# A separate order for the last visit of a two-layer graph kernel, and seven products for one output

## The chip, the cores and the metric

The kernel runs on one core of a Trainium2 chip. The metric is the device time in microseconds; 2795.61 is the median of three runs (2795.58 to 2795.65). A profiled execution of the same kernel took 2798.83.

## The reference

Sixty-four graphs of 256 nodes with 512 features go through two layers, all in fp32. Layer 0 is a graph attention with 8 heads of 64 units, layer 1 an attention with 8 heads whose weights are mixed with the adjacency. After each layer the input is added and the sum is normalized.

```python
# layer 0
feats = jnp.einsum('bnf,hfu->bhnu', X, W)
dense = leaky_relu(e_self[..., :, None] + e_neigh[..., None, :], 0.2) + NEG_BIG * (1.0 - A)
out = relu(einsum('bhij,bhju->bhiu', softmax(dense), feats) + b)
x = _layernorm(x + out)
# layer 1
qkv = (x @ W_qkv).reshape(B, N, HEADS, 3, DIM_HEAD)
attn = softmax(where(m2, q @ k.T * scale, -big)) * LA
attn = attn + LG * adj + LD * jnp.exp(-dist)     # adj and dist are both the adjacency
out = (attn @ v) @ W_out + b_out
x = _layernorm(x + out)
```

## The kernel before

Each graph is split in two row tiles of 128 nodes (T = 2) and four feature blocks of 128 (C = 4). Work of a graph is cut into stages (`turned`, `proj0`, `attend0`, `proj1`, `softmax1`, `attend1`), and each stage into named steps. `do(stage, graph, step)` (line 1240) emits one step and then calls `in_order`, which ties every instruction to the one before it on its engine. So the order of the `do` calls is the order of every engine's queue; nothing reorders it later.

Four graphs are in flight. For each graph b from 2 to 63 two functions are called: `attention0_beside_projections1` (line 1460) runs layer 0's attention of graph b beside the q/k and value projections of graph b-1 and the weighting of b-2; `attention1_beside_projections0` (line 1545) runs the rest of layer 1 of b-2, the scores of b-1 and layer 0's projections of b+1. After the loop `end` (line 1598) finishes graphs 60 to 63. For b = 63 the steps of the nonexistent graph 64 are skipped by `do`, so the loop's last visit keeps the loop's order with holes in it.

A projection is a 2 x 2 block product done in seven products instead of eight (`seven`, line 328). The products p1, p6, p7, p4 share one PSUM bank: each adds to it, and after each of them ScalarE (ACT) copies the bank out (`COPIES`, line 325), so the next of the four waits for that copy. p2 has a bank alone; p5 and p3 share one. VectorE (DVE) adds these banks to the copies (`add`: 11 after p1 and p2, 22 after p7 and p5, 12 after p3), and p3 must wait for the add 22 that reads its bank. The left factors of the seven products are differences of blocks (`left_factors`, line 307; for the output they are made in `half_blocks`, line 1116). All matmuls of a product go through `halved` (line 83), which writes 64 output rows at a time; row 87 of the profile is therefore shared by `pq_p` (q and k), `pv_p` (values), `pf_p` (layer 0) and `po_p` (output). The scores `pz` use 64 input rows (line 951), the row sums `pd` 32 output rows (line 988), `common` and `recs` the full array.

In layer 1 the exponentials run on ACT (line 972). The pair sums `both` run on DVE, row sums on TensorE (PE), and `invert` and `inverted` make reciprocals. A write to DRAM and a broadcast load bring them back as `rb` (1 MB, line 1039). `weights` (lines 1059 and 1068) then multiplies the exponentials by them and adds the common part. `values` (line 1078) multiplies with the value rows and ACT copies the result to `oT`. The last graph skips the broadcast: `last_values` computes the unscaled product `raw` and the part `common` apart, and `last_scaled` spreads the reciprocals with a matmul (`recs`).

In `end` of the kernel before, the output of graph 62 is not done in seven products but by rows: `project(t)` (line 1193) makes four blocks by two column groups for each row tile, then `sum_up` adds the input rows. Graph 63 does the same. The normalization takes the mean and three small operations on POOL (lines 385, 402, 405, 406), squares (391) and the scaling (410) on ACT, then a store on SP. `rows_again` (line 1088) loads the input rows of a graph back into `y`; graph 61's use the buffer of graph 60's output and so wait for its store. Buffers are tagged: one tag with `bufs=n` is a ring of n, and a step waits until the older user of its slot is done; `mm` (four PSUM slots) and `sc` (two large PSUM slots) are those that matter here.

Of the kernel before, what the change touches and what calls it, by code (L numbers as in the profile page):

```python
# [8 lines left out]
FT = mybir.dt.float32  # L9
# [8 lines left out]
def kernel(  # L18
# [49 lines left out]
    work = ctx.enter_context(tc.tile_pool(name="work", bufs=2))  # L68
# [858 lines left out]
    PROBS, REC = {}, {}  # L927

    def softmax1(b):
# [4 lines left out]
        both = {}  # L934
# [3 lines left out]
        def scores(g, part=None):  # L938

            if part is not None and part > 0:  # L940
                exponentials(g, PZ[g], {1: slice(0, None), 2: slice(0, -1), 3: slice(-1, None)}[part])
                return
            if g == 2 and b < NB - 1:
                pz = [ps_tile([P, T, N], f"pz_{b}_{g}_{r}") for r in range(2)]
            else:
                pz = psum.tile([P, 2, T, N], FT, tag="sc", name=f"pz_{b}_{g}", bufs=2)
                pz = [pz[:, r] for r in range(2)] + [pz]
            for j in range(T):
                for r in range(2):
                    rows = slice(r * U, (r + 1) * U)  # L950
                    matmul(  # L951
                        pz[r][:, j, :],
                        QK[b][rows, g, 1, j * P : (j + 1) * P],
                        QK[b][rows, g, 0, :],
                        start=True,
                        stop=True,
                    )
            if part == 0:
                PZ[g] = pz
                return  # L960
            exponentials(g, pz)
# [87 lines left out]
    def attend1(b):  # L1049
        if b < NB - 1:  # L1050
            oT = work.tile([P, C, N], FT, tag="oT", name=f"oT_{b}", bufs=1)
        else:
            oT = work.tile([P, C, N], FT, tag="xC", name=f"oT_{b}", bufs=1)
        av = {}

        def weights(g, step=None):
# [81 lines left out]
        def last_values():  # L1138

            raw = psum.tile([P, HG, N], FT, tag="sc", name="raw", bufs=2)  # L1140
            for g in range(HG):
                for j in range(T):
                    for r in range(2):
                        matmul(
                            raw[r * U : (r + 1) * U, g, :],
                            V1[b][:, j, 2 * g + r, :],
                            PROBS[b][g][:, r, j, :],
                            start=(j == 0),
                            stop=(j == T - 1),
                        )  # L1150
            for g in range(0, HG, 2):
                nc.scalar.copy(oT[:, g : g + 2, :], raw[:, g : g + 2, :])
            common = psum.tile([P, HG, N], FT, tag="sc", name="common", bufs=2)
            for g in range(HG):
                for j in range(T):
                    matmul(
                        common[:, g, :],
                        V1[b][:, j, 2 * g : 2 * g + 2, :].rearrange("p h u -> p (h u)"),
                        CT[b][:, j, :],
                        start=(j == 0),  # L1160
                        stop=(j == T - 1),
                    )
            LAST["common"] = common
            sel = work.tile([P, Q, U], FT, tag="gb", name="heads", bufs=1)
            nc.vector.tensor_copy(sel, ident[:, 0:P:B].unsqueeze(2).to_broadcast([P, Q, U]))
            LAST["sel"] = sel

        def last_scaled():

            for i in range(HG // 2):  # L1170
                both = slice(2 * i, 2 * i + 2)
                pr = ps_tile([P, 2, N], f"recs_{i}")
                for q in range(2):
                    matmul(
                        pr[:, q, :],
                        LAST["sel"][:, 2 * q : 2 * q + 2, :].rearrange("p k u -> p (k u)"),
                        REC[b][:, i, :],
                        start=True,
                        stop=True,
                    )  # L1180
                nc.vector.tensor_mul(oT[:, both, :], pr, oT[:, both, :])
                nc.vector.tensor_add(
                    oT[:, both, :], LAST["common"][:, both, :], oT[:, both, :]
                )

        def residual():
            if b == NB - 1:
# [20 lines left out]
        def store(ts=None):  # L1208
# [11 lines left out]
            residual=residual,  # L1220
            values=values,
            last_values=last_values,
            last_scaled=last_scaled,
            project=project,
            rows_again=rows_again,
# [234 lines left out]
    def attention0_beside_projections1(b):  # L1460
# [28 lines left out]
                do("attend0", b, "product", g, t)  # L1489
        do("attend0", b, "rec0", 0)  # L1490
        do("attend0", b, "rec0", 1)
        if b == 2:
            do("turned", 3, "xT")
            do("turned", 3, "xC")
# [103 lines left out]
    def end():  # L1598

        b = NB - 1  # L1600
        do("proj1", b, "qk", "p1")
# [8 lines left out]
        do("proj1", b, "qk", "p2")  # L1610
        do("proj1", b, "qk_add", 11)
        do("proj1", b, "qk", "p6")
# [8 lines left out]
        do("attend1", b - 1, "weights", 2)  # L1621
        do("attend1", b - 1, "weights", 3)
        do("attend1", b - 1, "values", 0)
        do("attend1", b - 1, "values", 1)
        do("attend1", b - 2, "residual")
        do("attend1", b - 2, "sum_up", 0)
        do("attend1", b - 2, "sum_up", 1)
        do("softmax1", b, "scores", 0)
        do("softmax1", b, "both", 0)
        do("softmax1", b, "scores", 1)  # L1630
        do("softmax1", b, "both", 1)
        do("proj1", b, "values", "p1")
        do("attend1", b - 2, "squares")
        do("attend1", b - 1, "residual")
        do("attend1", b, "residual")
        do("proj1", b, "values", "p2")
        do("proj1", b, "v_add", 11)
        do("attend1", b - 1, "values", 2)
        do("attend1", b - 1, "values", 3)
        do("softmax1", b, "scores", 2)  # L1640
        do("softmax1", b, "both", 2)
        do("softmax1", b, "scores", 3)
        do("softmax1", b, "both", 3)
        do("proj1", b, "values", "p6")
        do("attend1", b - 2, "store")
        do("proj1", b, "values", "p5")
        do("proj1", b, "values", "p7")
        do("proj1", b, "v_add", 22)
        do("proj1", b, "values", "p4")
        do("proj1", b, "values", "p3")  # L1650
        do("proj1", b, "v_add", 12)
        do("softmax1", b, "sums")
        do("softmax1", b, "invert")
        do("softmax1", b, "inverted")
        do("attend1", b, "last_values")
        do("attend1", b, "last_scaled")
# [4 lines left out]
        tiles = [slice(t, t + 1) for t in range(T)]  # L1661
# [62 lines left out]
```

## Time and profile before

| | us |
|---|---|
| median of the runs | 2795.61 |
| profiled execution, its own time | 2798.83 |
| its span, first to last instruction | 2796.9 |
| PE busy | 2778.1 (99%) |
| DVE busy | 2561.5 (92%) |
| ACT busy | 1794.7 (64%) |
| POOL busy | 417.0 (15%) |

The chain of work that ended last lies on PE for 97% of the span. A visit of the loop repeats about every 43 us: the first q/k product of a graph starts at 2649.70 for one and at 2692.39 for the next. The change begins at about 2705 us, after the last layer-0 attention product, so everything up to there is the same in both kernels. In a timeline row the columns are start, busy time, engine, line, operation, output and inputs, tile and number of records, and in brackets the idle time before it with what ended it. A matmul instruction leaves two records.

### The profile page before, as it was taken

How to read it: one execution, taken by the hardware profiler on the slowest of the kernel's cores; microseconds unless marked ns; L12 is line 12 of the kernel's file. 1: busy time of each engine (PE TensorE's matmuls, PEld its weight loads, DVE VectorE, ACT ScalarE, POOL GpSimd, SP SyncE). 2: the span in 40 equal slices, each digit the busy share in tenths (PEclk: the TensorE clock that was granted, in tenths of full speed). 3: DMA queues.
4: the chain of work that ended last, by engine and by line, in shares of the span. 5: the costliest groups of instructions: out<-in, count | busy, mean ns of one | idle time of the engine just before them, and what ended most of it. 6: DMA issues, size and time to landing. Idle time of an engine off the chain costs nothing.

```text
span 2796.9 us, 93442 instructions
## 1 busy us (share of the span) xinstructions
PE 2778.1 (99%) x38584; PEld 2201.3 (79%) x38584; DVE 2561.5 (92%) x5264; ACT 1794.7 (64%) x5051; POOL 417.0 (15%) x1031
## 2 busy tenths in 40 slices
PE   9999999999999999999999999999999999999998
PEld 7778778778788788888787877877877878778775
DVE  7899999999999999999999999999999999999984
ACT  4666666666666666666666666666666666666663
POOL 1111111111111111111111111111111111111111
PEclk9999999999999999999999999999999999999999
DMA  6444544545545445444454454454454544544531
GB/s 142 124 110 133 141 124 139 126 133 146 123 128 140 119 138 140 124 139 124 134 146 122 129 140 122 135 140 125 139 123 135 142 123 132 140 118 139 137 107 67
DMA packets 778388, 362.56 MB, mean 130 GB/s; under 512 B 694767, under 2 KB 696303, under 8 KB 761966
## 3 DMA queue, kind: packets, MB, share of 16 engines
q1 hardware_dynamic: 775854, 356.07, 47.7%
q8 instruction: 306, 5.01, 0.7%
q14 instruction: 116, 0.95, 0.1%
q10 hardware_dynamic: 2112, 0.52, 0.1%
HBM read 288.11 MB, written 68.13 MB: 127 GB/s over the span
## 4 chain that ended last, share of the span: by engine, by line
PE 97%; DVE 1%; ACT 1%; DMA 0%; issue 0%; POOL 0%; SPq 0%; DVEq 0%; POOLq 0%
PE pq_p L87 27%; PE po_p L87 14%; PE pf_p L87 13%; PE pv_p L87 13%; PE av L790 9%; PE pz L951 8%; PE av L1078 8%; PE pd L988 2%; PE po L87 1%; PE pf L87 0%; DVE p L1059 0%; DMA gb<-gs 0%; DVE p L1068 0%; PE pg L663 0%; ACT x L811 0%
## 5 line engine op out<-in xcount | busy, mean ns | idle before, releaser
L87 PE MATMUL pq_p<-hC,wqk_sb 128*64 128x128 f32 x8192 | 470.4, 273 | 1.7 <-ACT qk L348 1.5
L87 PEld LDWEIGHTS pq_p<-hC,wqk_sb 128*64 128x64 f32 x8192 | 448.7, 137 | 3.5 <-ACT qk L348 2.2
L767 DVE SCALAR_TENSOR_TENSOR pT<-gb,ccol,at 128x256 f32<-128x256 f32 x992 | 403.0, 478 | 17.2 <-ACT ccol L677 17.2
L87 PE MATMUL pq_p<-hT,wqk_sb 128*64 128x128 f32 x6144 | 357.9, 273 | 0.0
L972 ACT ACTIVATE p<-pz,hide 128x512 f32<-128x512 f32 x638 | 337.9, 621 | 30.3 <-PE pz L951 30.3
L87 PEld LDWEIGHTS pq_p<-hT,wqk_sb 128*64 128x64 f32 x6144 | 342.2, 137 | 9.8 <-issue 0.8
L1059 DVE TENSOR_TENSOR p<-p,rb 128x1024 f32<-128x1024 f32 x252 | 299.0, 1207 | 3.9 <-DMA rb<-rs 3.9
L1068 DVE TENSOR_TENSOR p<-p,ct 128x1024 f32<-128x1024 f32 x252 | 299.4, 1208 | 0.2
L811 ACT ACTIVATE x<-av,rec 128x64 f32<-128x64 f32 x1024 | 223.9, 334 | 62.2 <-DVE rec L803 62.2
L790 PE MATMUL av<-v,pT 128*64 128x65 f32 x8192 | 253.7, 222 | 1.7 <-issue 1.1
L87 PE MATMUL pf_p<-wf_sb,xC 128*64 128x264 f32 x1984 | 254.0, 386 | 0.1
L725 ACT ACTIVATE v<-v 128x64 f32<-128x64 f32 x1024 | 251.2, 336 | 3.8 <-DVE v L716 3.7
L790 PEld LDWEIGHTS av<-v,pT 128*64 128x64 f32 x8192 | 249.6, 138 | 4.2 <-issue 2.9
L402 POOL TENSOR_SCALAR rstd_l<-rstd_l 128x2 f32<-128x2 f32 (+1 forms) x130 | 95.0, 731 | 1054.9 <-ACT junk L391 1054.8
L87 PE MATMUL pv_p<-wv_sb,hC 128*64 128x256 f32 x2048 | 245.9, 381 | 2.4 <-ACT v L348 2.4
L348 ACT COPY qk<-pq_p 128x512 f32<-128x512 f32 x256 | 148.8, 581 | 154.6 <-PE pq_p L87 151.2
L348 ACT COPY v<-pv_p 128x256 f32<-128x256 f32 x256 | 95.4, 373 | 223.6 <-PE pv_p L87 223.5
L951 PE MATMUL pz<-qk 64*128 64x256 f32 x2048 | 238.6, 383 | 0.0
L87 PE MATMUL po_p<-wo_sb,oC 128*64 128x256 f32 x1984 | 235.3, 379 | 0.0
L1078 PE MATMUL av<-p,v 128*64 128x256 f32 x2016 | 229.4, 379 | 2.1 <-DVE p L1068 2.1
L951 PEld LDWEIGHTS pz<-qk 64*128 64x128 f32 x2048 | 192.4, 186 | 44.9 <-issue 24.8
L980 DVE SCALAR_TENSOR_TENSOR both<-p 128x512 f32<-128x512 f32 x256 | 172.9, 677 | 41.5 <-ACT p L972 41.3
(175 smaller groups left out, 4549.0 us busy)
## 6 DMA issues: line engine op xcount, KB each, us to landing
rb<-rs SPq DMA_DIRECT2D x63, 1024.0 KB
gb<-gs SPq DMA_DIRECT2D x62, 1028.0 KB
hs<-x SPq DMA_DIRECT2D x64, 512.0 KB
xb<-in_x_dram SPq DMA_DIRECT2D x252, 128.0 KB
x<-in_x_dram SPq DMA_DIRECT2D x63, 512.0 KB
y<-hs SPq DMA_DIRECT2D x63, 512.0 KB
out_dram<-y SPq DMA_DIRECT2D x63, 512.0 KB
hb<-hs SPq DMA_DIRECT2D x248, 128.0 KB
```

What stands on the lines that cost most here:

```text
L87: matmul(dst[cols], lhsT[:, cols], rhs, **flags)
L348: nc.scalar.copy(out[COPIES[p]], dst)
L725: nc.scalar.activation(v[:, :U], v[:, :U], AF.Copy, scale=v[:, U : U + 1])
L767: nc.vector.scalar_tensor_tensor(pT[h][:, j, :], GB[b][h], CCOL[b][:, j, h : h + 1], AT[b][:, j, :], op0=ALU.max, op1=ALU.mult,)
L790: matmul(av[r * half : (r + 1) * half, k, :], pT[h][:, j, i : i + half], V0[b][:, j, h, :UA], start=(j == 0), stop=(j == T - 1),)
L811: nc.scalar.activation(X1[b][:, t, h * U : (h + 1) * U], av[:, k, :U], AF.Copy, scale=REC0[g][:, t, k : k + 1],)
L951: matmul(pz[r][:, j, :], QK[b][rows, g, 1, j * P : (j + 1) * P], QK[b][rows, g, 0, :], start=True, stop=True,)
L972: nc.scalar.activation(to, of, AF.Exp, bias=hide[:, j, b : b + 1], scale=U**-0.5)
L980: nc.vector.scalar_tensor_tensor(both[g], p[:, :, 0, :], TINY, p[:, :, 1, :], op0=ALU.add, op1=ALU.add)
L1059: nc.vector.tensor_mul(p, p, REC[b][:, k : k + 2, g // 2, :] .unsqueeze(2) .to_broadcast([P, 2, T, N]),)
L1068: nc.vector.tensor_add(p, p, CT[b].unsqueeze(1).to_broadcast([P, 2, T, N]))
L1078: matmul(av[0][r * U : (r + 1) * U, g % 2, :], V1[b][:, j, 2 * g + r, :], PROBS[b][g][:, r, j, :], start=(j == 0), stop=(j == T - 1),)
```

## The change

The loop ends at graph 62. For graph 63 only the first half is called, and it returns after the reciprocals of its attention. `end` then holds all that follows in an order of its own, in which the products of graphs 61, 62 and 63 alternate more finely. The output of graph 62 goes through `half_blocks` and the seven products (so `oT` of graph 63 takes the buffer tag `hC`, as `xC` now holds the differences for 62). The `common` part of graph 63 becomes a step of its own, `last_common`, ahead of the row sums, and `last_scaled` takes the half to do as an argument. Score block 2 of graph 63 uses two `mm` slots, as in the other graphs.

```diff
-            if g == 2 and b < NB - 1:
+            if g == 2:
                 pz = [ps_tile([P, T, N], f"pz_{b}_{g}_{r}") for r in range(2)]
...
-            oT = work.tile([P, C, N], FT, tag="xC", name=f"oT_{b}", bufs=1)
+            oT = work.tile([P, C, N], FT, tag="hC", name=f"oT_{b}", bufs=1)
...
-            common = psum.tile([P, HG, N], FT, tag="sc", name="common", bufs=2)
+
+        def last_common():
+
+            common = LAST["common"] = psum.tile([P, HG, N], FT, tag="sc", name="common", bufs=2)
...
-        def last_scaled():
-
-            for i in range(HG // 2):
+        def last_scaled(i):
...
         do("attend0", b, "rec0", 1)
+        if b == NB - 1:
+            return
...
     def end():
         b = NB - 1
+        tiles = [slice(t, t + 1) for t in range(T)]
+        do("attend1", b - 2, "weights", 0, 0)
+        do("attend1", b - 2, "weights", 1, 0)
+        do("attend1", b - 2, "weights", 0, 1)
...
+        do("proj1", b - 1, "values", "p7")
+        do("proj1", b - 1, "v_add", 22)
+        do("attend0", b, "squares", tiles[1], slice(0, 2))
+        do("attend1", b - 2, "weights", 2, 1)
+        do("attend1", b - 2, "weights", 3, 0)
+        do("softmax1", b - 1, "scores", 0, 0)
+        do("proj1", b - 1, "values", "p4")
+        do("proj1", b - 1, "values", "p3")
+        do("proj1", b - 1, "v_add", 12)
+        do("attend1", b - 2, "weights", 3, 1)
+        do("attend0", b, "norm")
+        do("proj1", b, "blocks")
+        do("softmax1", b - 1, "scores", 1, 0)
+        do("attend1", b - 2, "values", 0)
+        do("softmax1", b - 1, "scores", 0, 1)
+        do("attend1", b - 2, "values", 1)
+        do("softmax1", b - 1, "scores", 1, 1)
+        do("softmax1", b - 1, "scores", 2, 0)
+        do("attend1", b - 3, "residual")
+        for t in range(T):
+            do("attend1", b - 3, "sum_up", t)
...
+        do("softmax1", b - 1, "sums")
+        do("attend1", b - 2, "product_add", 22)
+        do("softmax1", b - 1, "invert")
+        do("proj1", b, "hT")
+        do("softmax1", b - 1, "inverted")
+        do("attend1", b - 2, "product", "p4")
+        do("attend1", b - 2, "product", "p3")
         do("proj1", b, "qk", "p1")
+        do("proj1", b, "hC")
+        do("attend1", b - 2, "product_add", 12)
         do("attend1", b - 3, "squares")
+        do("proj1", b, "qk", "p2")
+        do("proj1", b, "qk_add", 11)
+        do("proj1", b, "qk", "p6")
         do("attend1", b - 3, "store")
...
         do("attend1", b - 1, "weights", 1)
+        do("proj1", b, "values", "p1")
         do("proj1", b, "qk", "p4")
         do("proj1", b, "qk", "p3")
         do("proj1", b, "qk_add", 12)
         do("attend1", b - 1, "weights", 2)
+        do("proj1", b, "values", "p2")
+        do("proj1", b, "v_add", 11)
+        do("proj1", b, "values", "p6")
+        do("proj1", b, "values", "p5")
+        do("proj1", b, "values", "p7")
+        do("attend1", b - 2, "residual")
+        do("proj1", b, "v_add", 22)
...
         do("attend1", b - 1, "values", 0)
         do("attend1", b - 1, "values", 1)
+        do("proj1", b, "values", "p4")
+        do("proj1", b, "values", "p3")
+        do("attend1", b - 2, "squares")
         do("softmax1", b, "scores", 0)
+        do("softmax1", b, "scores", 1)
+        do("proj1", b, "v_add", 12)
+        do("softmax1", b, "scores", 2, 0)
+        do("attend1", b - 1, "values", 2)
+        do("attend1", b - 1, "values", 3)
...
+        do("attend1", b, "last_common")
+        do("softmax1", b, "sums")
+        do("softmax1", b, "invert")
+        do("attend1", b, "last_values")
+        do("softmax1", b, "inverted")
...
-        do("attend1", b - 1, "project", 0)
-        do("attend1", b - 1, "project", 1)
+        do("attend1", b - 1, "product", "p1")
+        do("attend1", b - 1, "product", "p2")
+        do("attend1", b - 1, "product_add", 11)
+        do("attend1", b - 1, "product", "p6")
+        do("attend1", b, "last_scaled", 0)
+        do("attend1", b - 1, "product", "p5")
+        do("attend1", b - 1, "product", "p7")
+        do("attend1", b - 1, "product_add", 22)
+        do("attend1", b, "last_scaled", 1)
+        do("attend1", b - 1, "product", "p4")
+        do("attend1", b - 1, "product", "p3")
+        do("attend1", b - 1, "product_add", 12)
+        for t in range(T):
+            do("attend1", b - 1, "sum_up", t)
         do("attend1", b - 1, "squares")
         do("attend1", b - 1, "store")
...
-    for b in range(2, NB):
+    for b in range(2, NB - 1):
         attention0_beside_projections1(b)
         attention1_beside_projections0(b)
+    attention0_beside_projections1(NB - 1)
     end()
```

More of the change, by code (lines that the diff above doesn't have):

```diff
@@ L1162, in last_values @@
                     )
-            LAST["common"] = common
             sel = work.tile([P, Q, U], FT, tag="gb", name="heads", bufs=1)
@@ L1166, in last_values @@
             LAST["sel"] = sel
-        def last_scaled():
-            for i in range(HG // 2):
[L1171 to L1183, printed above, removed]
-                )
+        def last_scaled(i):
+            both = slice(2 * i, 2 * i + 2)
+            pr = ps_tile([P, 2, N], f"recs_{i}")
+            for q in range(2):
+                matmul(
+                    pr[:, q, :],
+                    LAST["sel"][:, 2 * q : 2 * q + 2, :].rearrange("p k u -> p (k u)"),
+                    REC[b][:, i, :],
+                    start=True,
+                    stop=True,
+                )
+            nc.vector.tensor_mul(oT[:, both, :], pr, oT[:, both, :])
+            nc.vector.tensor_add(
+                oT[:, both, :], LAST["common"][:, both, :], oT[:, both, :]
+            )
         def residual():
@@ L1222, in attend1 @@
             last_values=last_values,
+            last_common=last_common,
             last_scaled=last_scaled,
@@ L1600, in end @@
         b = NB - 1
+        tiles = [slice(t, t + 1) for t in range(T)]
[3 more added lines that the diff above has]
+        for t in range(T):
+            do("attend0", b, "norm0", 0, t)
+        do("proj1", b - 1, "qk", "p4")
+        for t in range(T):
+            do("attend0", b, "norm0", 1, t)
+        do("proj1", b - 1, "qk", "p3")
+        do("attend1", b - 2, "weights", 1, 1)
+        do("proj1", b - 1, "qk_add", 12)
@@ new lines, in end @@
+        do("attend0", b, "end")
+        do("proj1", b - 1, "values", "p1")
+        do("proj1", b - 1, "values", "p2")
+        do("proj1", b - 1, "v_add", 11)
+        do("attend1", b - 2, "weights", 2, 0)
+        do("proj1", b - 1, "values", "p6")
+        do("attend0", b, "squares", tiles[0], False)
+        do("proj1", b - 1, "values", "p5")
+        do("proj1", b - 1, "values", "p7")
+        do("proj1", b - 1, "v_add", 22)
+        do("attend0", b, "squares", tiles[1], slice(0, 2))
+        do("attend1", b - 2, "weights", 2, 1)
@@ new lines, in end @@
+        do("softmax1", b - 1, "scores", 1, 1)
+        do("softmax1", b - 1, "scores", 2, 0)
+        do("attend1", b - 3, "residual")
+        for t in range(T):
+            do("attend1", b - 3, "sum_up", t)
+        do("attend1", b - 2, "values", 2)
+        do("attend1", b - 2, "values", 3)
+        do("attend1", b - 2, "half_blocks", 0)
+        do("softmax1", b - 1, "both", 0)
+        do("attend1", b - 2, "half_blocks", 1)
+        do("softmax1", b - 1, "both", 1)
+        do("softmax1", b - 1, "scores", 2, 2)
@@ new lines, in end @@
+        do("softmax1", b - 1, "scores", 3, 0)
+        do("attend1", b - 2, "product", "p1")
+        do("softmax1", b - 1, "scores", 2, 3)
+        do("softmax1", b - 1, "scores", 3, 1)
+        do("softmax1", b - 1, "both", 2)
+        do("softmax1", b - 1, "both", 3)
+        do("attend1", b - 2, "product", "p2")
+        do("attend1", b - 2, "product_add", 11)
+        do("attend1", b - 2, "product", "p6")
+        do("attend1", b - 2, "product", "p5")
+        do("attend1", b - 2, "product", "p7")
@@ L1609, in end @@
         )
-        do("proj1", b, "qk", "p2")
-        do("proj1", b, "qk_add", 11)
-        do("proj1", b, "qk", "p6")
         do("attend1", b - 1, "weights", 0)
@@ L1621, in end @@
         do("attend1", b - 1, "weights", 2)
+        do("proj1", b, "values", "p2")
[5 more added lines that the diff above has]
+        do("proj1", b, "v_add", 22)
+        for t in range(T):
+            do("attend1", b - 2, "sum_up", t)
         do("attend1", b - 1, "weights", 3)
@@ L1624, in end @@
         do("attend1", b - 1, "values", 1)
-        do("attend1", b - 2, "residual")
-        do("attend1", b - 2, "sum_up", 0)
-        do("attend1", b - 2, "sum_up", 1)
+        do("proj1", b, "values", "p4")
+        do("proj1", b, "values", "p3")
+        do("attend1", b - 2, "squares")
         do("softmax1", b, "scores", 0)
+        do("softmax1", b, "scores", 1)
[3 more added lines that the diff above has]
+        do("attend1", b - 1, "values", 3)
@@ L1629, in end @@
+        do("softmax1", b, "scores", 2, 1)
+        do("softmax1", b, "scores", 3)
         do("softmax1", b, "both", 0)
-        do("softmax1", b, "scores", 1)
         do("softmax1", b, "both", 1)
-        do("proj1", b, "values", "p1")
-        do("attend1", b - 2, "squares")
+        do("attend1", b - 2, "store")
+        do("attend1", b - 1, "half_blocks", 0)
+        do("attend1", b - 1, "half_blocks", 1)
+        do("softmax1", b, "both", 2)
+        do("softmax1", b, "both", 3)
+        do("attend1", b, "last_common")
@@ L1634, in end @@
+        do("softmax1", b, "sums")
+        do("softmax1", b, "invert")
+        do("attend1", b, "last_values")
+        do("softmax1", b, "inverted")
         do("attend1", b - 1, "residual")
         do("attend1", b, "residual")
[L1636 to L1655, printed above, removed]
@@ L1656, in end @@
-        do("attend1", b, "last_scaled")
-        do("attend1", b - 1, "project", 0)
-        do("attend1", b - 1, "project", 1)
+        do("attend1", b - 1, "product", "p1")
[6 more added lines that the diff above has]
+        do("attend1", b - 1, "product_add", 22)
@@ L1659, in end @@
+        do("attend1", b, "last_scaled", 1)
+        do("attend1", b - 1, "product", "p4")
+        do("attend1", b - 1, "product", "p3")
+        do("attend1", b - 1, "product_add", 12)
+        for t in range(T):
+            do("attend1", b - 1, "sum_up", t)
         do("attend1", b - 1, "squares")
         do("attend1", b - 1, "store")
-        tiles = [slice(t, t + 1) for t in range(T)]
         for t in range(T):
```

## The prediction

> **What bounds the kernel now.** I read the page's first part, then, for the stretch that the change rewrites (2,700 us to the end), the waits of PE, PE's timeline and the table of stretches.
>
> ```profile
> span 2796.9 us, 93442 instructions
> PE 2778.1 (99%) x38584; PEld 2201.3 (79%) x38584; DVE 2561.5 (92%) x5264; ACT 1794.7 (64%) x5051; POOL 417.0 (15%) x1031
> ```
>
> PE is busy 99% of the span, so a gain is either fewer matmuls or less PE idling. The waits of PE from 2,700 us on (total, times, longest):
>
> ```profile
> PE pv_p L87 <- ACT v L348: 3.4, 3, 2.4
> PE av L1078 <- DVE p L1068: 2.1, 2, 1.6
> PE pq_p L87 <- ACT qk L348: 1.0, 2, 0.7
> ```
>
> 6.5 us of idling in the last 97 us, a third of PE's 18.8 in the whole span. PE's timeline where the longest sits (start, busy time, records; two records make one matmul instruction):
>
> ```profile
> 2755.29 1.95 PE L87 MATMUL pv_p<-wv_sb,hC 128*64 128x256 f32 x16
> 2759.66 1.98 PE L87 MATMUL pv_p<-wv_sb,hC 128*64 128x256 f32 x8 [2.42 <-ACT v L348]
> 2762.11 1.98 PE L87 MATMUL pv_p<-wv_sb,hT 128*64 128x256 f32 x8 [0.47 <-ACT v L348]
> 2763.87 1.92 PE L87 MATMUL pv_p<-wv_sb,hC 128*64 128x256 f32 x8
> 2765.72 1.29 PE L988 MATMUL pd<-both,ones 128*32 128x256 f32 x16
> ```
>
> Eight such records take 0.86 us elsewhere (2708.18 to 2709.91 is sixteen); here 1.8. The table of stretches says why (length, busy times of PE, PEld, DVE, ACT, POOL, then the granted clock):
>
> ```profile
> 2746.00:2757.00 11.00, 11.00 (x100) 7.21 (x96) 10.84 (x15) 5.34 (x12) 0.95 (x2) 1.00 0.23 86
> 2757.00:2759.60 2.60, 0.24 (x4) 0.00 (x0) 1.90 (x4) 2.60 (x7) 1.81 (x3) 0.96 0.00 0
> 2759.60:2761.70 2.10, 1.98 (x8) 0.77 (x8) 0.47 (x1) 1.43 (x4) 0.00 (x0) 0.50 0.00 0
> 2764.00:2766.00 2.00, 2.00 (x14) 0.79 (x14) 0.16 (x1) 0.37 (x1) 0.00 (x0) 0.50 0.00 0
> 2770.00:2776.00 6.00, 6.00 (x32) 4.70 (x30) 0.72 (x2) 1.07 (x2) 0.00 (x0) 1.00 0.00 0
> ```
>
> After the 2.42 us stall the clock is 0.50 for some 6 us.
>
> **The change part by part.** For the waits I laid the new queue of each engine end to end with the durations of these rows, from the point where both kernels part; the positions in brackets below come from that.
>
> *Stalls removed.* The profile counts idling from a matmul's end (0.379 us after its start), while matmuls follow each other every 0.216 us; so each of the seven stalls loses 0.17 us more than is printed: 6.5 + 7 x 0.17 = 7.7 us. Why each goes: in a product chain p6, p7, p4 the same bank is copied out by ACT (0.37 us for v, 0.59 for qk) before the next product may write it. Graph 62's p7 and p4 now have score block 0 (1 us) between them, graph 63's value p7 and p4 have two AV blocks (1.73), its q/k p7 and p4 the value p1 (0.86), and ACT copies p6 ahead of the normalization of graph 60 (1.5 us), which stood before it. The 2.42 us stall was that copy queued behind two squares, the oT copy and four exponentials; in the new order the v copies precede the exponentials of graph 63. The AV stall (2.1 us) was DVE being late with weights 2 and 3 of graph 61; now the residual and two sums (1.2 + 2 x 0.6 us) come after them, and PE reaches AV 2 and 3 some 4 us later behind p4, p3 and score blocks 0, 1 and 2, so weights 3 is done about 3 us early.
>
> *Half clock gone.* Three products at 1.8 instead of 0.86 us, less two restarts and a shape border (0.2), and pd 1.23 for 1.00: 2.7 us. Here a rule is to be weighed. The Trainium skill, "TensorE: Matmul & The Clock Gate", Part 1, lets PE fall to half clock after an idle window of about 3.4 us; by that, 2.42 us should have cost nothing and removing it would be worth 0, the sum 5.4. The row shows 0.50 after 2.42 us, while 1.57 us (before 2719.96) left it at 1.00. I take the row: 2.7. In the new order I find no stall above 0.8 us, so neither gives a new half-clock spell.
>
> *Seven products for eight.* The output of graph 62 was 2 x 16 matmuls, 2 x 3.45 us (2775.93 to 2782.88); seven products of four are 6.05: 0.9 us less. Their four ACT copies (0.37), three adds and four half-block differences on DVE (0.42 each) stand beside PE: DVE is idle for most of the last 25 us.
>
> *More changes of tile shape.* This speaks against the change: "TensorEngine Tiling (Array Packing)", Key Properties, has a switch of tiling mode drain TensorE. It states no price; taken as nothing, the sum would be 9.5. The rows of a visit in mid-run:
>
> ```profile
> 2677.76 3.62 PE L1078 MATMUL av<-p,v 128*64 128x256 f32 x32
> 2681.32 3.73 PE L951 MATMUL pz<-qk 64*128 64x256 f32 x32
> 2684.97 1.95 PE L87 MATMUL po_p<-wo_sb,oT 128*64 128x256 f32 x16
> 2686.75 2.76 PE L87 MATMUL po_p<-wo_sb,oC 128*64 128x256 f32 x24
> ```
>
> Starts are 3.56, 3.65 and 1.78 apart, where 32, 32 and 16 records at 0.108 make 3.46, 3.46 and 1.73: one excursion into the score shape costs 0.10 + 0.19 + 0.05 = 0.34 us; the full shape (common, recs) likewise (raw 3.60, common 3.56, recs 1.82 for 3.46, 3.46, 1.73). Before there are four such excursions in the tail (scores 62; scores 63 twice; common with recs). After there are nine (62's blocks singly, 63's as three and one, common, recs twice), of which scores-common-row sums share two borders: 5 x 0.34 - 0.25 = 1.45 us lost. Bounds: 1.0 (short blocks drain less) to 2.9 (double).
>
> *A new stall at hT.* The transpose hT of graph 63 now follows "invert" on DVE instead of the second "both". Counted from the start of the last row-sum matmul: it ends 0.39 us later, DVE takes 0.71 + 0.24 + 0.17 + 1.24 and some hand-overs, so hT is there after 2.8; PE is through border (0.37), p4 and p3 (1.73) after 2.1: 0.7 us lost at the first q/k product of 63. Bounds 0.4 to 1.2. The hb load is not what it waits for: x_63 is normalized some 3 us earlier than at 2718.71, so hb, for which DVE waited until 2728.08, lands near 2725, and DVE asks near 2729.4.
>
> *The end.* Two projections of graph 63 (6.9 us) follow the output of 62 in both kernels, but the first row tile of 62 was summed beside the second (2779.72), and now an add (0.44) and both sums come after the last product: 62's mean starts 1.05 us later against PE. It had 0.1 us to spare: its two squares (1.75), POOL's three (1.45) and two normalizations (1.45) ended at 2788.60 in front of tile 0 of 63 on ACT and POOL, and that tile's chain ended at 2790.60 when tile 1's mean was due at 2790.80. So 0.95, taken as 1.0 us lost; bounds 0.7 to 1.1.
>
> *Sum.* 7.7 + 2.7 + 0.9 - 1.45 - 0.7 - 1.0 = 8.1 us. Span 2796.9 becomes 2788.8, the profiled execution's own 2798.83 becomes 2790.7, and the median of the runs, 3.2 below it, 2795.61 - 8.1 = 2787.5.
>
> *At nothing, with their cover:* SP keeps its order of loads and stores; the sum over all heads (common) moves ahead of the row sums with its inputs long there. Weights 0 of graph 62 waits for rb (5.1 us from issue); qk_add 22 is queued behind it on DVE, and the q/k p3 waits for that: cover about 0.8 us, then 1:1. The residual of 61 waits for y_61, whose load (3.7 us) waits for the store of y_60 (landed 3.95 us after issue); behind the residual on DVE stands v_add 22, for which value p3 waits on PE: cover about 2.4 us.
>
> **The rivals.** *(a) The change doesn't do what it says:* every wait comes back elsewhere, and only products and borders count: 0.9 - 1.45 = -0.55, 2796.2. Against: the stalls have three named causes, each with work put between. *(b) One stall returns or the shapes cost double:* rb 2 us late (1.2), or the y_61 chain, or 1.45 more for borders: 2788.7 to 2790.7. For it: covers of 0.7 to 0.8 us at rb and at the second row sums. *(c) Slower:* the residual of 61, moved ahead of v_add 22. Load and store both slower beyond the 2.4 us stop PE one for one, and past 2 us of stall the half clock takes 2.7 more. It decides from 2.4 + (8.1 - 2.7) = 7.8 us late: over 2795.6; at 13.4 late, 2801.2. Against: store and load took 7.6 us together while rb was still landing (until 2740.69); they would have to double. *(d) The half-clock spell is the profiled execution's own*, as the clock page's window would have it, and the timed runs lack it: gain 5.4, 2790.2.
>
> **How the numbers follow.** A change of 0.2%, 5.6 us, is about what a measurement tells from none: the border is 2790.0. Forecast 0.72, its own range 2786.2 to 2789.0 (hT 0.4 to 1.2, borders 1.0 to 2.1, end 0.7 to 1.1); (b) 0.13, two in three of it under 2790.0; (d) 0.06; (a) 0.06; (c) 0.03. Faster: 0.72 + 0.09 + a third of (d), 0.83. Same: 0.04 + 0.04 + 0.06, 0.14. Slower 0.03. The range holds the forecast, (b) and half of (d): 2785.8 to 2790.6.
>
> **What would show it.** PE's waits from 2,700 us on: none of the three lines above, one at pq_p behind DVE of 0.5 to 1 us; granted clock 1.00 in every 2 us up to the last matmul; last matmul about 9 us earlier, then 5 us to the end of the last ACT row instead of 4.0 (2789.97 to 2793.93). pz in blocks of 8 records with the next start 0.2 to 0.35 us later than the record count. Wrong if a stall over 2 us appears (clock 0.50 after it), if PE waits at pv_p for v_add 22 or at pq_p for qk_add 22, or if the exponentials of 62 hold up the row sums.

## The result, and the profile after

| | before | after |
|---|---|---|
| median of 18 runs each, us | 2796.14 (2793.90 to 2798.17) | 2788.84 (2787.43 to 2792.14) |
| profiled execution, its own time / span | 2798.83 / 2796.9 | 2792.14 / 2790.3 |
| last matmul ends, us from the span's start | 2789.96 | 2782.53 |

The ratio is 0.9974, 95% interval 0.9967 to 0.9982: 7.3 us faster, between 5.0 and 9.2. The prediction was 2787.5 in a range of 2785.8 to 2790.6, so 2788.84 lies inside it, 1.3 above the value.

Two traces cannot be laid over each other from their starts: the code up to 2,705 us is the same, yet "after" reaches that place 2.2 us later. I therefore measure from a common mark, the first matmul of graph 62's q/k product p4 (2704.68 before, 2706.90 after), to the end of the last ACT row, and call it the tail. The tail went from 89.25 to 80.50 us, 8.75 less (forecast 8.1): PE's part from 85.28 to 75.63, and the part after PE's last matmul from 3.97 to 4.88.

First the head of the page after, then the waits of PE from 2,700 us on (total, times, longest):

```profile
span 2790.3 us, 93433 instructions
PE 2776.2 (99%) x38576; PEld 2198.7 (79%) x38576; DVE 2565.0 (92%) x5271; ACT 1796.6 (64%) x5057; POOL 417.3 (15%) x1031
```

```profile
PE pq_p L87 <- DVE hT L130: 0.8, 1, 0.8
```

The page looks the same, PE busy 99%; eight PE records are gone (seven products for eight). The waits show the change: the three lines of before are gone and one new one stands, 0.8 us. PE's and DVE's timeline around it (start, busy time, in brackets the idle time before and its cause):

```profile
2730.30 0.72 DVE L1010 STREAM_TRANSPOSE zd<-pd 128x512 f32<-128x512 f32 x1 [0.19 <-PE pd L988]
2731.05 0.25 DVE L1016 RECIPROCAL inv<-zd 128x16 f32<-128x16 f32 x1
2731.34 0.19 DVE L1020 TENSOR_TENSOR inv<-inv,rowmask 128x16 f32<-128x16 f32 x1
2731.52 1.25 DVE L130 STREAM_TRANSPOSE hT<-hb 128x1024 f32<-128x1024 f32 x1
2732.91 3.71 PE L87 MATMUL pq_p<-hT,wqk_sb 128*64 128x128 f32 x64 [0.80 <-DVE hT L130]
```

DVE makes hT only after the transpose and the two operations of `invert`, and PE has run out of products by then. The table of stretches where the clock had dropped (length, busy times of PE, PEld, DVE, ACT, POOL, then the granted clock):

```profile
2746.00:2757.00 11.00, 11.00 (x104) 7.55 (x102) 9.27 (x14) 5.02 (x12) 2.22 (x4) 1.00 0.23 84
2757.00:2760.00 3.00, 3.00 (x21) 2.03 (x18) 2.36 (x7) 2.75 (x8) 0.00 (x0) 1.00 0.02 5
2760.00:2764.00 4.00, 4.00 (x34) 2.69 (x34) 1.94 (x4) 2.49 (x4) 0.00 (x0) 1.00 0.15 57
```

PE is busy through, at 1.00. Last, ACT's rows at the end:

```profile
2780.88 1.52 ACT L410 ACTIVATE y<-y,shift_l,rstd_l 128x512 f32<-128x512 f32 x2 [1.37 <-POOL shift_l L406]
2782.31 0.71 ACT L391 ACTIVATE junk<-x,nmean_l 128x512 bf16<-128x512 f32 x1
2784.53 0.72 ACT L391 ACTIVATE junk<-x,nmean_l 128x512 bf16<-128x512 f32 x1 [1.43 <-POOL nmean_l L385]
2786.59 0.81 ACT L410 ACTIVATE x<-x,shift_l,rstd_l 128x512 f32<-128x512 f32 x1 [0.54 <-POOL shift_l L406]
```

The same rows in the kernel before:

```profile
2787.17 1.52 ACT L410 ACTIVATE y<-y,shift_l,rstd_l 128x512 f32<-128x512 f32 x2 [1.37 <-POOL shift_l L406]
2788.60 0.71 ACT L391 ACTIVATE junk<-x,nmean_l 128x512 bf16<-128x512 f32 x1
```

In both kernels the normalization of graph 62 (y, x2) comes first and the squares of graph 63's tile 0 (x) follow at its end. But in the kernel before it ended at 2788.69, 1.3 us ahead of the last matmul; now it ends at 2782.40, 0.1 ahead, so graph 62 stands in the way of graph 63.

**Where PE's 9.65 us (85.28 - 75.63) came from.** In both traces I summed, over the matmul instructions of the tail, what each start-to-start distance has above the pace of its kind (0.216 us for a 256-column instruction). A stall counts with the 0.17 us that the profile does not print, called its issue time below. The 7.70 are 7.06 at six stalls and 0.64 (0.47 printed and 0.17 of issue) at the seventh, which fell into the half clock. The clock's part is taken by difference with the runs that lack it, below.

| part of the tail | forecast, us | measured, us |
|---|---|---|
| stalls, 7.70 before | -7.7 | -7.70 |
| new stall at hT | +0.7 | +0.97 |
| half clock | -2.7 | -2.7 |
| seven products for eight | -0.9 | -0.86 (four instructions at 0.216) |
| shape changes and restarts, net | +1.45 | +0.64 (what is left of PE's 9.65) |
| from the last matmul to the end | +1.0 | +0.91 |
| sum | -8.1 | -8.74 (the tails: 8.75) |

### The profile page after: what moved, and what is told of

Same layout as the page of the kernel before. It is cut to its first block, busy times and chain, and to the rows that moved or that the text cites. A ratio compares the mean times of both kernels' runs of the same rounds, so it can differ in the third digit from the quotient of the medians.

```text
span 2790.3 us, 93433 instructions
## 1 busy us (share of the span) xinstructions
PE 2776.2 (99%) x38576; PEld 2198.7 (79%) x38576; DVE 2565.0 (92%) x5271; ACT 1796.6 (64%) x5057; POOL 417.3 (15%) x1031
## 4 chain that ended last, share of the span: by engine, by line
PE 97%; DVE 1%; DMA 1%; SPq 1%; ACT 1%; issue 0%; POOL 0%; ACTq 0%; DVEq 0%; POOLq 0%
PE pq_p L87 28%; PE po_p L87 14%; PE pf_p L87 14%; PE pv_p L87 14%; PE av L790 9%; PE pz L951 8%; PE av L1078 8%; PE pd L988 2%; SPq L273 0%; SPq L123 0%; DMA gb<-gs 0%; DMA wf_sb<-in_L_gnn_W_dram 0%; DMA wk<-in_L_gnn_W_qkv_dram 0%; ACT x L811 0%; PE pg L663 0%
## 5 line engine op out<-in xcount | busy, mean ns | idle before, releaser
L972 ACT ACTIVATE p<-pz,hide 128x512 f32<-128x512 f32 (+1 forms) x640 | 338.4, 620 | 29.3 <-PE pz L951 29.3
```

The lines of the kernel that those rows point to most:

```text
L972: nc.scalar.activation(to, of, AF.Exp, bias=hide[:, j, b : b + 1], scale=U**-0.5)
```

## The experiments

My theory: the gain is the stalls and the half clock, and both went because products were woven between the waits; the seven products are nearly nothing. Rivals: a better order on ACT or DVE alone gives the same; the seven products or the new shapes matter; the half clock is a feature of one execution.

All tails in one table (mark to the end of the last ACT row), then each run.

| run | mark | PE's part | after PE | tail |
|---|---|---|---|---|
| before | 2704.68 | 85.28 | 3.97 | 89.25 |
| e0 before again | 2704.64 | 85.02 | 3.97 | 88.99 |
| e2 p6 early | 2704.04 | 85.34 | 3.98 | 89.32 |
| e7 ACT freed | 2703.20 | 79.92 | 3.97 | 83.89 |
| e8 DVE freed | 2702.66 | 83.75 | 3.97 | 87.72 |
| e9 both freed | 2704.82 | 81.16 | 3.97 | 85.13 |
| after | 2706.90 | 75.63 | 4.88 | 80.50 |
| e11 after again | 2704.70 | 75.63 | 4.88 | 80.51 |
| e1 output by rows | 2704.45 | 76.14 | 3.98 | 80.12 |
| e3 hT early | 2705.58 | 74.62 | 4.90 | 79.51 |
| e4 scores together | 2704.77 | 75.28 | 4.90 | 80.18 |
| e5 store later | 2703.20 | 75.63 | 3.97 | 79.60 |
| e6 e3, e4 and e5 | 2704.73 | 74.45 | 3.97 | 78.41 |
| e10 e1, e3 and e4 | 2705.03 | 74.90 | 3.97 | 78.87 |

A tail repeats well: 80.50 and 80.51 for two executions of "after", 89.25 and 88.99 for two of "before".

### The kernel before, unedited

> The kernel before, unchanged. Measured is the tail: from the start of graph 62's q/k p4 to the end of the last ACT row, 89.25 us in the profile of before (2704.68 to 2793.93). If the half-clock spell belongs to the order of the work, a stall of 2.4 us before the value p7 of graph 63 and a granted clock of 0.50 for 6 to 7 us appear again, and the tail is 89.2 within 0.7. If the spell was that one execution's own, the clock stays 1.00 and the tail is about 86.5. The part ahead of the tail (2704.68 us then) shows how much it wanders between executions of equal code.

The waits came back to the digit (pv_p 3.4, av 2.1, pq_p 1.0) and so did the half clock, but in two places of one window each. PE's timeline and the stretches of this run:

```profile
2717.26 1.08 PE L1078 MATMUL av<-p,v 128*64 128x256 f32 x8 [0.49 <-DVE p L1068]
2719.91 1.59 PE L1078 MATMUL av<-p,v 128*64 128x256 f32 x8 [1.57 <-DVE p L1068]
```

```profile
2720.00:2724.00 4.00, 4.00 (x22) 2.60 (x24) 1.19 (x3) 1.67 (x4) 0.00 (x0) 0.57 0.35 131
2760.00:2762.00 2.00, 1.16 (x8) 0.58 (x8) 0.79 (x2) 2.00 (x4) 0.15 (x1) 0.83 0.00 0
2762.00:2764.00 2.00, 1.53 (x8) 0.75 (x8) 0.42 (x1) 0.57 (x2) 0.00 (x0) 0.50 0.44 169
```

The clock fell after the 1.57 us stall, which in the first profile left it at 1.00, and again after the 2.43 us one. Both profiled executions of the kernel before thus lost two windows, but not in the same place.

### One product moved: p6 early

```diff
         do("attend1", b - 1, "values", 3)
+        do("proj1", b, "values", "p6")
         do("softmax1", b, "scores", 2)
...
         do("softmax1", b, "both", 3)
-        do("proj1", b, "values", "p6")
         do("attend1", b - 2, "store")
```

> The kernel before with one step moved: the value product p6 of graph 63 stands ahead of score blocks 2 and 3, so ACT's copy of its bank is queued before their four exponentials. If the stall of 2.42 us and the half clock after it are one cause, both go: the stall is 0.5 us or less, the clock 1.00, the tail 89.25 - (2.0 to 2.4) - 2.7 = 84.3 within 0.5, the time some 4.9 us below before. If the half clock has another cause (for instance low activity over a longer stretch), only the stall goes: clock 0.50 somewhere after 2,755 us, tail 87.0, time 2.2 us below before.

A miss: tail 89.32, and the time ratio of 12 runs 1.0000 (0.9992 to 1.0009). PE's and ACT's timeline of this run:

```profile
2756.33 0.37 ACT L348 COPY v<-pv_p 128x256 f32<-128x256 f32 x1
2756.59 2.44 ACT L972 ACTIVATE p<-pz,hide 128x512 f32<-128x512 f32 x4
2758.89 1.54 ACT L410 ACTIVATE y<-y,shift_l,rstd_l 128x512 f32<-128x512 f32 x2
2760.30 0.39 ACT L348 COPY v<-pv_p 128x256 f32<-128x256 f32 x1
2760.74 1.97 PE L87 MATMUL pv_p<-wv_sb,hT 128*64 128x256 f32 x8 [2.90 <-ACT v L348]
```

The copy of p6 is prompt now, but the next copy, of p7, stands behind the same four exponentials and, in place of the squares, the normalization of graph 61: the stall moved on by one product, 2.90 us instead of 2.42. Moving one member of a chain of copies moves the wait.

### ACT freed: p6 early and graph 61's normalization out of the way

```diff
         do("proj1", b, "values", "p1")
-        do("attend1", b - 2, "squares")
...
         do("attend1", b - 1, "values", 3)
+        do("proj1", b, "values", "p6")
...
-        do("proj1", b, "values", "p6")
-        do("attend1", b - 2, "store")
...
         do("softmax1", b, "invert")
+        do("attend1", b - 2, "squares")
+        do("attend1", b - 2, "store")
         do("softmax1", b, "inverted")
```

> The kernel before with ACT's queue freed in front of the value copies of graph 63: p6 ahead of score blocks 2 and 3, and the squares and the normalization of graph 61 behind the row sums. The run with p6 alone moved left the stall in place, because the copy of p7 still stood behind four exponentials (2.44 us) and a normalization (1.54). If that queue is the cause, the stalls at pv_p behind ACT fall from 3.4 us to 1.0 or less, no half clock follows them, and the tail (start of graph 62's q/k p4 to the end of the last ACT row, 89.0 to 89.3 before) is 84.2 to 85.7, the upper end if the stall at AV behind DVE (2.1 us, untouched) brings one half-clock window of 3.4 us as in the second profile of before. If the stalls wander on to another wait, the tail stays within 1 us of 89.1.

Tail 83.89, 5.4 us of the 8.75 by a reorder on one engine, 0.3 below the expected span. Its waits of PE:

```profile
PE av L1078 <- DVE p L1068: 2.1, 2, 1.6
PE pq_p L87 <- ACT qk L348: 1.0, 2, 0.7
PE pv_p L87 <- ACT v L348: 0.9, 2, 0.5
```

The stalls cost 5.11 us against 7.70, so 2.6 of the 5.4 are stalls; no half clock is in this trace, and I put the other 2.8 down to that.

### DVE freed in the loop's last visit

```diff
-        do("attend1", b - 3, "residual")
+        if b < NB - 1:
+            do("attend1", b - 3, "residual")
...
-        for t in range(T):
+        for t in range(T) if b < NB - 1 else ():
             do("attend1", b - 3, "sum_up", t)
...
         do("attend1", b - 2, "weights", 3, 1)
         do("proj0", b + 1, "add", 12)
+        if b == NB - 1:
+            do("attend1", b - 3, "residual")
+            for t in range(T):
+                do("attend1", b - 3, "sum_up", t)
```

> The kernel before with only DVE's order changed in the last visit: the residual and the two sums of graph 60 come behind weights 3 of graph 61. If these 2.4 us of DVE work are what makes AV 2 and 3 of graph 61 wait, the 2.1 us of stall at AV behind DVE go and the tail is 86.5 to 87.2 (2.1 + 2 x 0.17 us less, half clock at the end unchanged). If DVE is late for another reason (the load rb, or its sheer amount of work), half or more of the stall stays: 88 or above.

Tail 87.72, worse than expected, and the reason for the gain is not the expected one either. The waits of PE, and PE's timeline at the long stall:

```profile
PE pv_p L87 <- ACT v L348: 3.5, 3, 2.4
PE pq_p L87 <- ACT qk L348: 1.0, 2, 0.7
PE av L1078 <- DVE p L1068: 1.0, 1, 1.0
PE pd L988 <- DVE both L980: 1.0, 1, 1.0
PE pz L951 <- ACT p L972: 1.0, 1, 1.0
```

```profile
2758.84 1.08 PE L87 MATMUL pv_p<-wv_sb,hC 128*64 128x256 f32 x8 [2.43 <-ACT v L348]
2760.52 1.08 PE L87 MATMUL pv_p<-wv_sb,hT 128*64 128x256 f32 x8 [0.59 <-ACT v L348]
```

The AV stall halved, but the 2.4 us of freed DVE work came to lie where the exponentials and the pair sums of graph 62 are wanted, and two new stalls of 1.0 appeared: the waits are 7.5 us, 1.0 more than before, and with their issue time the stalls cost 8.91 us against 7.70. So the gain of 1.5 is the clock's: after a stall of 2.43 us eight records take 1.08 here and not 1.98.

### Both freed

The diff is the two above together.

> Both edits on the kernel before. If the two stalls are independent and the half clock follows from them, the tail is about 82.0 to 82.6: 89.1 - 2.4 (AV) - 2.0 (net of a rest at pv_p) - 2.7 (half clock), and the clock is 1.00 throughout. That would be six sevenths of the change's gain with four moved steps. If the weaving is needed to hide the waits that remain, the tail is 84 or more.

Tail 85.13, 1.2 worse than with ACT freed alone. PE's waits at av, pd and pz, 1.0 us each, are those of the run with DVE freed; at pv_p 0.9 of its 3.5 us are left. DVE has no room in that visit: in these runs what left one wait made another. In "after" score blocks and AV blocks lie between, and the residual costs no wait. No run wove PE's products alone, with ACT and DVE as they were.

### The output of graph 62 by rows again

```diff
-        do("attend1", b - 1, "half_blocks", 0)
-        do("attend1", b - 1, "half_blocks", 1)
...
-        do("attend1", b - 1, "product", "p1")
-        do("attend1", b - 1, "product", "p2")
-        do("attend1", b - 1, "product_add", 11)
-        do("attend1", b - 1, "product", "p6")
+        do("attend1", b - 1, "project", 0)
         do("attend1", b, "last_scaled", 0)
-        do("attend1", b - 1, "product", "p5")
-        do("attend1", b - 1, "product", "p7")
-        do("attend1", b - 1, "product_add", 22)
         do("attend1", b, "last_scaled", 1)
-        do("attend1", b - 1, "product", "p4")
-        do("attend1", b - 1, "product", "p3")
-        do("attend1", b - 1, "product_add", 12)
-        for t in range(T):
-            do("attend1", b - 1, "sum_up", t)
+        do("attend1", b - 1, "project", 1)
```

> The changed kernel with the output of graph 62 by rows again (two row tiles of sixteen matmuls, both recs products between them, no half-block differences). If my sum holds, the seven products are worth 0.86 us on PE but cost 0.95 at the end, because the add and both sums come after the last product: PE's last matmul comes 0.5 us later than in the changed kernel (0.86 less one shape excursion of 0.34), the tail behind the last matmul is 4.0 us instead of 4.9, and the whole tail is 80.1 against 80.5 of the changed kernel. If the products are a gain of their own, the tail is 80.9 to 81.4.

Tail 80.12: PE ends 0.51 later (the products' 0.86 less one excursion to recs, which by rows come in one block), and the end takes 3.98 instead of 4.88. Together that is 0.38 less than with seven products: this part of the change did not make the kernel faster as it was placed.

### hT ahead of the reciprocals

```diff
         do("attend1", b - 2, "product_add", 11)
+        do("proj1", b, "hT")
         do("attend1", b - 2, "product", "p6")
...
         do("softmax1", b - 1, "invert")
-        do("proj1", b, "hT")
```

> The changed kernel with the transpose hT of graph 63 moved on DVE from behind invert to behind the first output add of graph 61, where its load has landed (2728.7 in the changed kernel's profile). If hT's place behind the row sums is the whole cause of PE's one stall (0.80 us printed, 0.97 of issue time), the stall goes and the tail is 80.5 - 0.9 = 79.6. If the load is the limit, DVE waits there for hb, the row sums and the broadcast rb come later, and PE stalls at the q/k p3 instead: tail 80.3 to 81.

Tail 79.51, no wait of PE left in it: the 0.80 us wait with its issue time is worth 0.99.

### One excursion less: score block 2 of graph 62 beside block 3

```diff
         do("softmax1", b - 1, "scores", 1, 1)
-        do("softmax1", b - 1, "scores", 2, 0)
         do("attend1", b - 3, "residual")
         for t in range(T):
             do("attend1", b - 3, "sum_up", t)
         do("attend1", b - 2, "values", 2)
         do("attend1", b - 2, "values", 3)
+        do("softmax1", b - 1, "scores", 2, 0)
```

> The changed kernel with score block 2 of graph 62 moved behind AV 2 and 3 of graph 61, next to block 3: one excursion into the score shape fewer. If an excursion costs what I took from the rows, the tail is 80.50 - 0.34 = 80.16 and PE's last matmul comes 0.34 us earlier against the start of the tail. If the border price is hidden or nil, nothing moves (80.5). If the exponentials of block 2, now 2.9 us later, hold up the row sums, the tail is 80.6 to 81.5.

Tail 80.18: 0.32 less for one excursion into the score shape and out (PE's part is 0.35 shorter). The rows of "after" show the same (starts 2714.81, 2715.87, 2716.79: 1.06 and 0.92 where eight records make 0.86):

```profile
2714.81 1.13 PE L951 MATMUL pz<-qk 64*128 64x256 f32 x8
2715.87 1.08 PE L87 MATMUL pv_p<-wv_sb,hT 128*64 128x256 f32 x8
2716.79 1.03 PE L87 MATMUL pv_p<-wv_sb,hC 128*64 128x256 f32 x8
```

### The store of graph 62 behind tile 0's squares

```diff
         do("attend1", b - 1, "squares")
-        do("attend1", b - 1, "store")
         for t in range(T):
             do("attend1", b, "project", t)
             do("attend1", b, "squares", tiles[t])
+            if t == 0:
+                do("attend1", b - 1, "store")
```

> The changed kernel with the normalization and store of graph 62 moved behind tile 0's squares of graph 63. My theory: after the last matmul 4.88 us pass instead of 3.97 because the three small POOL operations and two ACT normalizations of graph 62 stand in front of tile 0 of graph 63 on both engines, so tile 1, the last, starts late. With them behind, 3.9 to 4.0 pass; PE's part stays 75.6 and the tail (first q/k product p4 of graph 62 to the end of the last ACT row) is 79.5 to 79.6 against 80.50. Rival: the late mean of graph 62 on DVE (sums after the last product instead of one beside the second row) is itself what comes last, or the delayed store only moves the queue to the end; then the tail stays 80.3 to 80.6.

Tail 79.60, and 3.97 after the last matmul. ACT's rows of this run:

```profile
2777.38 0.72 ACT L391 ACTIVATE junk<-x,nmean_l 128x512 bf16<-128x512 f32 x1 [1.57 <-POOL nmean_l L385]
2778.10 1.50 ACT L410 ACTIVATE y<-y,shift_l,rstd_l 128x512 f32<-128x512 f32 x2
2779.93 0.72 ACT L391 ACTIVATE junk<-x,nmean_l 128x512 bf16<-128x512 f32 x1 [0.32 <-POOL nmean_l L385]
```

Tile 0's squares (x) now come before graph 62's normalization (y), which fills the time in which POOL works for graph 63. The order of two steps was the whole 0.9.

### The three together, and the same by rows

The diff of the first is that of the last three runs; of the second, the output by rows with the edits of hT and of score block 2.

> The changed kernel with three moves at once: hT behind the first output add of graph 61 (0.99 us in its own run), score block 2 of graph 62 beside block 3 (0.32), the store of graph 62 behind tile 0's squares of graph 63 (0.9). If they add up, the tail is 80.50 - 2.2 = 78.2 to 78.4 us, and the time about 2.2 us under that of the changed kernel, 9.5 us under the kernel before (ratio 0.9966, with both kernels' scatter of 2 us round it). If they share a cover (the same wait hides two of them), the tail is 79.2 to 79.5.

> The changed kernel with the output of graph 62 by rows again (as in the kernel before) and hT and score block 2 moved as in the run with all three moves. It asks whether seven products are worth anything once the end of the kernel is in order. My theory, 0.9 us for seven products on PE: tail 80.12 - 0.99 - 0.32 = 78.8, 0.5 longer than with seven products and the store moved. Rival: the seven products' extra waits and shapes eat the 0.9; then 78.2 to 78.4, the same as there.

Tails 78.41 and 78.87: the three moves add up (2.09 of 2.2), and with the end in order the seven products are worth 0.46. Five runs each on one chip: 2787.90 (2787.74 to 2788.51) and 2788.84 (2787.49 to 2789.45), against 2798.68 before, ratios 0.9964 (0.9951 to 0.9976) and 0.9965 (0.9952 to 0.9979). That the version with the three moves beats "after" rests on the tails, which repeat to 0.3; the intervals of the times overlap.

### The changed kernel again

> The changed kernel once more, unedited, for two questions. First, whether the 0.8 us late start of its own profile (full clock at 10.5 us instead of 4 to 7, everything upstream some 2 us later) is that one execution's own: then the tail is 80.5 again, but its mark (first q/k product p4 of graph 62) lies at 2703 to 2705.5 and not at 2706.9, and the span at 2786.5 to 2789. Second, what the half clock is worth over many executions: if it were a fixed 2.7 us of the kernel before, the changed kernel would be 8.5 to 9 us faster in the median, as the tails are; if it comes in some executions of the kernel before only, the executions before fall into a group of mean clock 0.998 and one of 0.999 that differ by some 2 us, those of the changed kernel show 0.999 to 1.0 alone, and the medians differ by 6.5 to 9.5 depending on how many of each there are. Against the kernel with the three moves (tail 78.4) the same ratio to before should be 0.0007 higher, 0.9971.

Mark 2704.70, tail 80.51, span 2788.2: the late mark of the first profile was that execution's own. Six runs have a median of 2789.09 against 2797.66, ratio 0.9968 (0.9956 to 0.9980): 8.6 us, where the first comparison gave 7.3. None of the runs of "after" or its variants shows a mean granted clock of 0.998; of 35 listed runs of before 11 do (median 2798.73) and 24 show 0.999 (2797.19). But the two groups overlap (2797.30 to 2800.17 and 2795.60 to 2800.85), and in the ten runs of this comparison they are not apart at all, so the mean clock does not explain the scatter of single runs.

## Why the prediction was right, and where a step was off

*Stalls removed, 7.7.* Right, also in the 0.17 us per stall that the profile does not print: the tail's excess at stalls is 7.70 before. That it needed weaving was argued from three causes; the three reorders without it fall short. ACT's order alone gives the long stall back (2.6), DVE's order takes 1.2 more in stalls than it gives, and from the best of these (83.89) to "after" 3.4 remain: 4.1 of stalls and 0.9 of products, less 0.7 of shapes and 0.9 at the end.

*Half clock gone, 2.7.* For the profiled execution the size was right: in the three runs of before's variants without it the tail is shorter by 2.6 to 2.8 than the difference of their stalls gives (5.36 - 2.59, 1.53 + 1.21, 4.12 - 1.48). The reading was not. I set the row (0.50 after 2.42 us, 1.00 after 1.57) against the idle window of 3.4 us of the Trainium skill, "TensorE: Matmul & The Clock Gate", Part 1, and took the row for a threshold on the length of one stall. In the repeat the clock fell after 1.57, and with DVE freed it stayed at 1.00 after 2.43. Of the four profiled executions with a stall of 2.4 to 2.9 us there, three lost two windows in their tail and one none.

For the timed runs 2.7 was probably too much, so rival (d) may hold in part. Every one of the fourteen traces ends with 2.4 to 4.8 us at half clock, when PE has finished. By an estimate from these, two lost windows (6.83 us) on top of that make a mean clock of 0.998, and one or none makes 0.999 or 1.000. Then 11 of the 35 listed runs of before lost two and the others one at most: 0.8 to 1.8 us on average.

*Seven products, 0.9; the end, 1.0.* Measured 0.86 and 0.91, both right; e1 and e5 show them apart. As the change stood they cancelled each other. The end was taken as given with the order; it was the place of one step.

*Shapes, 1.45.* This term was right. The price per excursion was forecast at 0.34 and e4 shows 0.32; summed over the instructions of the tails, the shape changes cost 1.96 us before and 3.43 after, 1.47 more. The net is 0.64 because the waits that went took small things along that stood at nothing in the sum: a late second instruction after a restart (0.05 each, some 0.25 in all) and a pause of 0.42 within the row sums of graph 62, whose last pair sum came from DVE only at 2729.90. (The 0.16 left over is within what the half clock's 2.7 is known to.) Those row sums and the product behind them, before and then after, are 1.42 and 1.00 apart:

```profile
2729.09 1.49 PE L988 MATMUL pd<-both,ones 128*32 128x256 f32 x16
2730.51 1.08 PE L87 MATMUL po_p<-wo_sb,oT 128*64 128x256 f32 x8
```

```profile
2729.16 1.07 PE L988 MATMUL pd<-both,ones 128*32 128x256 f32 x16
2730.16 1.08 PE L87 MATMUL po_p<-wo_sb,oT 128*64 128x256 f32 x8
```

The rule that spoke against the change (the Trainium skill, "TensorEngine Tiling (Array Packing)", Key Properties) is borne out in so far as a switch costs time: 0.10 us at the first instruction of the new shape, and at its second 0.10 in the score or the full shape, 0.05 on the way back to 128*64 and 0.02 in the row sums.

*hT, 0.7.* Measured 0.97 (bounds 0.4 to 1.2): mis-sized by its issue time, 0.17, which I had charged to the old stalls and not to the new one, and by 0.1 of hand-overs on DVE.

*At nothing.* PE waited neither at v_add 22 nor at qk_add 22, so rivals (b) and (c) did not come. Both transfers came in their cover.

*The value.* By the tails the gain was 8.75 instead of 8.1. By the medians it is 7.3 and 8.6 in two comparisons, whose intervals (5.0 to 9.2, 5.6 to 12.3) hold both. Of the 1.3 us between 2787.5 and 2788.84, 0.5 is the kernel before, 2796.14 over 18 runs where three had given 2795.61. The other 0.8 is within the scatter of medians, but the half clock accounts for it as well: with 0.8 to 1.8 us in the place of 2.7 the 8.75 become 6.9 to 7.8. By this estimate the forecast came so close partly by luck: 0.65 too little for the tail stood against 0.9 to 1.9 too much for the clock.

## What to carry to other kernels

When a chain of products waits for copies on another engine, look at what stands in that engine's queue ahead of every copy of the chain; here moving one product only handed the wait to the next. On an engine as full as DVE (92% busy) moving work away from one wait made others, as long as nothing else was put where it landed. After a reorder, look at the last few rows: here 0.9 us hung on which of two graphs was normalized first, as much as the saved eighth product.

## What the runs showed of the hardware

**The clock works in windows of 3.41 us.** In all fourteen traces each spell of granted clock after the first rise, at 1.00 or 0.50, is a multiple of 3.413 us long (but for the last, cut by the end): 6.827 at 0.50 in "before", twice 3.413 in its repeat. Laid on that grid, the idle time of PE in one window and the clock in the next are:

| run | window starts at | clock in it | PE idle in it, us | clock in the next |
|---|---|---|---|---|
| before | 2718.43 | 1.00 | 1.52 | 1.00 |
| e7 | 2715.65 | 1.00 | 1.74 | 1.00 |
| e0 | 2716.93 | 1.00 | 1.90 | 0.50 |
| e2 | 2756.32 | 1.00 | 2.01 | 0.50 |
| e8 | 2755.02 | 1.00 | 2.02 | 1.00 |
| before | 2755.98 | 1.00 | 2.16 | 0.50 |
| e0 | 2757.89 | 1.00 | 2.43 | 0.50 |
| e0 | 2761.31 | 0.50 | 0.47 | 1.00 |
| before | 2759.39 | 0.50 | 0.74 | 0.50 |
| e2 | 2759.73 | 0.50 | 1.01 | 0.50 |

So in these runs it is not one stall's length that counts but the idle time that falls into one window, from about 1.9 to 2.0 us on; the 2.02 us of e8 shows that the border is not sharp in this measure. The same 2.43 us stall falls whole into a window or is cut by its edge (2.02 and the rest in e8), and two stalls can add up (1.57 and 0.33 of the 0.49 in e0, where "before" has the 0.49 in another window). At half clock a window with 0.74 and one with 1.01 us of idle time were followed by another at half clock, one with 0.47 was not. This agrees with the free-running window of the Trainium skill, "TensorE: Matmul & The Clock Gate", Part 1 (4096 cycles at 1.2 GHz, 3413 ns); that the window must be idle, as its table has it, these runs do not bear out.

**The start.** The first rise to full clock came between 3.9 and 7.0 us in thirteen traces and at 10.5 us in that of "after", whose mark is 2.2 us behind its repeat's (rise at 5.3). There the eight matmuls of line 434 started 0.4 us later than in the repeat (behind a load) and took 3.75 us instead of 2.10, and at 12 us the lag of 2.2 is there already, so this one is accounted for. The marks of the others still spread from 2702.66 to 2705.58 with identical code up to there, and what sets that was not tried.
